# Routing the first part of a mixture-of-experts kernel over six token columns instead of eight

## The chip, the cores and the metric

The kernel runs on one core of one Trainium2 chip. The metric is the device time of one execution in microseconds (us). Three executions of the kernel before took 511.5, 511.85 and 511.92 us; their median is 511.85 us. A profile is a further execution, recorded instruction by instruction; its own time is given beside its span, which runs from the first to the last instruction.

The engines are named as in the profile: PE is the matrix engine (TensorE), with PEld for its weight loads; DVE is VectorE, ACT is ScalarE, POOL is GpSimd, and SP is the engine whose queue issues most transfers.

## The reference

There are 4096 tokens of 256 numbers (64 rows of 64 tokens), eight experts, and two experts chosen for each token. Cut to what matters:

```python
var = jnp.mean(x * x, axis=-1, keepdims=True)
xn = rms_w * (x * jax.lax.rsqrt(var + EPS))
gate = xn @ wg_W + wg_b + (genre_embed @ gg_W + gg_b)
gate_w = jax.nn.softmax(gate, axis=-1)
topk_w, topk_i = jax.lax.top_k(gate_w, TOP_K)          # TOP_K = 2 of E = 8
cw = jnp.sum(jax.nn.one_hot(topk_i, E) * topk_w[..., None], axis=-2)
h1 = jax.nn.relu(jnp.einsum('bsh,ehm->bsem', x, W1) + b1)      # 256 -> 512
h2 = jax.nn.relu(jnp.einsum('bsem,emn->bsen', h1, W2) + b2)    # 512 -> 512
out_e = jnp.einsum('bsen,enh->bseh', h2, W3) + b3              # 512 -> 256
x = x + jnp.einsum('bseh,bse->bsh', out_e, cw)
```

The reference computes all experts for all tokens. Only the two chosen experts of a token have a weight other than zero, so 8192 pairs of token and expert matter.

## The kernel before, in words

**Layout.** Partition p of the 128 holds tokens 32p to 32p+31. Token column i is the i-th token of every partition, that is 128 tokens; there are NI = 32 columns, in groups of TPB = 4, and NG = 8 groups. x is loaded in groups: `load_x(j)` brings group j into `big`. Six groups fit at once; the last two go where groups 0 and 1 were, once these have been used.

**Sorting into tiles.** The pairs are sorted by expert into tiles of BT = 128 pairs, each tile of one expert. A tile is then computed by a gather of its rows of x (an indirect transfer on POOL), three layers on PE with ACT's activations between them, and a scatter that adds the weighted result to the output rows.

**Two parts.** Finding the tiles of all tokens takes long, so the kernel routes the first NA = 8 columns alone first (part A: 1024 tokens, 2048 pairs). From these, each expert gets one first tile of 128 pairs, listed in `idxA`. While PE computes these eight first tiles (`head_step`, one tile each), DVE routes the other NB = 24 columns (part B), and puts what is left of part A and all of part B into the remaining tiles, listed in `idxR`. How many of them are needed depends on the data: 56 to 69, and the last few are behind a switch. A tile in `idxR` is one of a pair of equal expert (two tiles at once, 256 columns on PE) or a single one.

**The front, in the order of the program** (`first_part`). Everything is written in program order under a manual schedule: each engine takes its instructions in the order in which the code names them, and waits are put in from what reads and writes which tile. A PSUM bank (`PB[k]`) counts as one object in this.

1. x groups 0 and 1 are loaded, transposed on PE (`turn`: `turn_pe` writes a bank, `turn_copy` copies it to SBUF on ACT or DVE). `squares(i, eng)` sums the squares of column i into `ss[:, i]`, on ACT (L185) or DVE (L187). Of the eight columns, ACT takes 2, 3, 6, 7 and DVE takes 0, 1, 4, 5. Column 6 stands ahead of the copy of the fourth transposed block on ACT, column 7 behind it.
2. `gates_2` multiplies the transposed columns by the gate weights on PE (L227). ACT copies the result to `gTs` (L448).
3. `pA.norm` makes one over the root mean square from `ss` (L288 to L299, with the square root on ACT, L290).
4. `upright_2` turns the gates so that tokens stand on partitions again, into bank `PB[4]` (L233), four columns to each half. ACT then copies a transposed block (L209), converts half of a table of numbers to float16 (`row_numbers`, L245), and copies three more transposed blocks of the later groups.
5. `pA.choose` is a chain of DVE operations. It reads the bank and multiplies by `rstd` (L308), adds the condition's gates (L315), finds the largest and second largest of each token with a scan (L322), an equality (L331), a difference (L334) and a masking (L337), and counts the pairs along a partition (L342, `incA`). Each works on n·E = 8·8 = 64 elements per partition.
6. `pA.ranks` adds the counts over the partitions on PE (L348, L349), DVE makes each pair's place in its expert's list (L476, L358, L360, `lo16A`).
7. Places are turned to token numbers by one-hot matmuls: 16 columns (2 choices by 8 token columns) in four groups of four, DVE makes each group (L484, `ohA`), PE uses it (L488). DVE makes `idxA` of the result (L492, L493).
8. `gather(0)` on POOL (L712) fetches the first tile's rows; PE transposes them (L767) and starts layer one (L831). On SP, the loads of the weights from the third of expert 0 on wait for this gather (`other_loads`), so that the first tile's rows go first.

**Part B** (`rest`) is a generator. `head_step` takes pieces of it between the steps of the first tiles; its DVE lines are those of part A with n = 24. The two copies of L539 and L544 bring its gates from PSUM into `graw` (32 columns by 8), from which `pB.choose(None)` multiplies.

**Other users of NA.** The sums of squares of the later columns are taken from the list `left`; the weights of the pairs go to `cwdA` (part A; the other columns of it are filled with zeros early, L422) and `cwdR`; and the output is first filled with x: columns 0 to NA-1 in one transfer (L509), the others in four (L929), so that scatters of the first eight tiles may start early.

Of the kernel before, what the change touches and what calls it, by code (L numbers as in the profile page):

```python
# [10 lines left out]
F16 = mybir.dt.float16  # L11
# [10 lines left out]
def kernel(  # L22
# [28 lines left out]
    MC = M // P  # L51
    REP = P // B
    TOPK = 2
    NA = 8
    GA = NA // TPB
    NB = NI - NA
    BT = 128
    SQ = 32
# [22 lines left out]
    def buf(pool, shape, name, dt=F32):  # L81
        return pool.tile(shape, dt, tag=name, name=name)
# [77 lines left out]
    def t2(name, n, dt=F32):  # L160
        return buf(gx, [P, n], name, dt)
# [90 lines left out]
    class Part:  # L252
# [48 lines left out]
        def choose(self, raw):  # L301

            gate, left, rstd = self.gate, self.pr[:, 0], self.t["rstd"]
            if raw is None:
                V.tensor_tensor(gate, graw[:, self.i0 : self.i1, :], self.over_e(rstd), ALU.mult)
            else:
                q = raw.shape[1]
                V.tensor_tensor(  # L308
                    gate.rearrange("p (q k) e -> p q k e", q=q),
                    raw,  # L310
                    self.over_e(rstd).rearrange("p (q k) e -> p q k e", q=q),
                    ALU.mult,
                )
            yield
            V.tensor_tensor(gate, gate, self.over_i(ggate), ALU.add)  # L315
            yield
            gf = gate.rearrange("p i e -> p (i e)")
            tops = (self.pr[:, 1], self.cw8.rearrange("p i e -> p (i e)"))
            ms = []
            for k, (g, top) in enumerate(zip((gf, left), tops)):  # L320

                V.tensor_tensor_scan(  # L322
                    top, fresh[:, 0 : self.n].rearrange("p i e -> p (i e)"), g, 0.0, ALU.add, ALU.max
                )
                top = top.rearrange("p (i e) -> p i e", e=E)
                m = top[:, :, E - 1]
                ms.append(m)
                yield
                if k == 0:
                    nc.gpsimd.tensor_tensor(self.w, gate, self.over_e(m), ALU.subtract)  # L330
                V.tensor_tensor(self.same[:, :, 1:], top, self.over_e(m), ALU.is_equal)  # L331
                yield
                oh = self.ohe[:, k].rearrange("p e i -> p i e")
                V.tensor_tensor(oh, self.same[:, :, 1:], self.same[:, :, 0:E], ALU.subtract)  # L334
                yield
                if k == 0:
                    V.scalar_tensor_tensor(  # L337
                        left.rearrange("p (i e) -> p i e", e=E), oh, -BIG, gate, ALU.mult, ALU.add
                    )
                    yield  # L340

            V.tensor_tensor_scan(self.inc[:, 1:], self.oh[:, 0], self.oh[:, 1], 0.0, ALU.add, ALU.add)  # L342
            V.tensor_tensor(self.t["d2"], ms[1], ms[0], ALU.subtract)
# [34 lines left out]
            nc.gpsimd.dma_start(cwd.rearrange("(p i) e -> p i e", p=P)[:, i0 : i0 + cw8.shape[1], :], cw8)  # L378

    pA, pB = Part("A", 0, NA), Part("B", NA, NI)  # L380
    lo16A = t2("lo16A", GC, F16)
    mvA = buf(gx, [P, GC, E], "mvA", F16)
    totA, totA1 = te("totA"), t2("totA1", E + 1)
    sa, sb = t2("sa", NREST), t2("sb", NREST)

# [9 lines left out]
            loads.append(nc.sync.dma_start(dst, src))  # L395


    left = [NA + i for i in (0, 1, 4, 5, 2, 3, 6, 7)] + list(range(NA + 8, NI))

    def some(n):  # L400
        for _ in range(n):
# [2 lines left out]
    def first_part():  # L404


        rw2 = gTs[0:HC, 0:P]
        load_x(0)
        nc.scalar.dma_start(wg_in, wg_W.rearrange("(c p) e -> p c e", p=P))
        load_x(1)  # L410
        nc.scalar.dma_start(rw2, rms_w.rearrange("(c p) -> c p", c=HC))
        load_x(2, 2)
        nc.scalar.dma_start(gg_sb[0:G, :], gg_W)
        load_x(4, 2)
        nc.scalar.sqrt(warm, ones[:, 0:E])
        V.memset(wg_sb, 0.0)
        V.memset(condT[G : G + 2, :, :], 1.0)
        V.memset(cw8B, 0.0)
        for k in range(3):
            V.memset(ring(run, [P, H], "xg", 3, k), 0.0)  # L420
        V.memset(cgR, 0.0)
        nc.gpsimd.dma_start(cwdA.rearrange("(p i) e -> p i e", p=P)[:, NA:NI, :], cw8B[:, NA:NI, :])  # L422
        busy(7)
        rwp, cps, gps = PB[7][:, P : P + HC], PB[7][0:G, 2 * P : 2 * P + B], PB[7][:, 3 * P : 3 * P + E]
        nc.tensor.transpose(rwp, rw2, ident[:HC, :HC])
        V.tensor_copy(rwT, rwp)
        for c in range(HC):
            V.tensor_scalar(wg_sb[:, c, 0:E], wg_in[:, c, :], rwT[:, c : c + 1], None, ALU.mult)
        for i in (2, 3):
            squares(i, "A")  # L430
        turn(0, 0, 0, "V", 0)
        turn(0, 1, 1, "A", 1)
        squares(0, "V")
        turn(1, 0, 2, "V", 2)
        squares(TPB + 2, "A")
        turn(1, 1, 3, "A", 3)
        squares(TPB + 3, "A")
        nc.tensor.transpose(cps, cond_sb, ident[:B, :B])
        for i in (1, TPB, TPB + 1):
            squares(i, "V")  # L440
        V.tensor_copy(condT[0:G], cps.unsqueeze(2).to_broadcast([G, B, REP]))
        for j in range(NG - GA, NG):
            load_x(j)
        nc.sync.dma_start(vecs[0 : E * MC, :], b1.rearrange("e (c p) -> (e c) p", p=P))
        nc.sync.dma_start(vecs[E * MC : 2 * E * MC, :], b2.rearrange("e (c p) -> (e c) p", p=P))
        load_weights(0, (0, 1))
        gates_2(((0, 1), (2, 3)), PB[3])
        nc.scalar.copy(gTs, PB[3])  # L448
        pA.norm(True)
        turn(GA, 0, 0, "A", 0)  # L450
        nc.tensor.matmul(gps, lhsT=condT.rearrange("g b r -> g (b r)"), rhs=gg_sb, start=True, stop=True)
        V.tensor_copy(ggate, gps)
        row_numbers(0)
        chosen = pA.choose(upright_2(PB[4]))
        for q in (1, 2, 3):
            turn(GA + q, 0, q, "A", q)
        turn_pe(GA, 1, 0)
        next(chosen)
        turn_pe(GA + 1, 1, 4)
        for _ in chosen:  # L460
            pass
        pA.ranks()
        V.tensor_tensor(
            mvA.rearrange("p (k i) e -> p k i e", k=TOPK),
            pA.ohe.rearrange("p k e i -> p k i e"),
            toka.unsqueeze(1).unsqueeze(3).to_broadcast([P, TOPK, NA, E]),
            ALU.mult,
        )
        row_numbers(1)
        pA.exps()  # L470
        gates(0, range(4))
        turn_pe(GA + 2, 1, 1)
        turn_copy(0, "A", 0)
        turn_copy(1, "A", 4)
        turn_copy(2, "A", 1)
        V.scalar_tensor_tensor(  # L476
            pA.slot, pA.inc[:, 1:].rearrange("p (e i) -> p e i", e=E), -1.0, pA.along(pA.adj), ALU.add, ALU.add
        )
        pA.pick(lo16A.rearrange("p (k i) -> p k i", k=TOPK))
        tabA = PB[7][:, 0:E]  # L480
        GH = GC // 4
        for g0 in range(0, GC, GH):
            hs = slice(g0, g0 + GH)
            V.tensor_tensor(  # L484
                ohA[:, :, hs], iotx[:, :, hs], lo16A[:, hs].unsqueeze(1).to_broadcast([P, P, GH]), ALU.is_equal
            )
            for g in range(g0, g0 + GH):
                nc.tensor.matmul(tabA, lhsT=ohA[:, :, g], rhs=mvA[:, g, :], start=(g == 0), stop=(g == GC - 1))  # L488
        pA.totals()
        turn(GA + 3, 1, 3, "A", 2)  # L490

        V.tensor_scalar(sa[:, 0:E], tabA, 0.0, float(NT), ALU.is_equal, ALU.mult)  # L492
        V.scalar_tensor_tensor(idxA, tabA, float(OFFA), sa[:, 0:E], ALU.add, ALU.add)  # L493
        V.tensor_copy(totA1, pA.tot)

    def other_loads():
# [9 lines left out]
        load_weights(1, (0,))  # L506
        nc.sync.dma_start(b3_sb[:, 0:2], b3[0:2].unsqueeze(0).to_broadcast([P, 2, H]))
        load_weights(1, (1, 2))
        fills.append(nc.sync.dma_start(our[:, 0:NA, :], xr[:, 0:NA, :]))  # L509
        load_weights(2)  # L510
        nc.sync.dma_start(b3_sb[:, 2:E], b3[2:E].unsqueeze(0).to_broadcast([P, E - 2, H]))
        for e in range(3, E):
# [21 lines left out]
    def third_part():  # L534

        turn(GA + 5, 1, 7, "V", 3)
        some(len(left))
        raw = upright()
        nc.scalar.copy(graw[:, NA : NA + 4 * TPB, :].rearrange("p (q k) e -> p q k e", q=4), raw)  # L539
        gates_2(((4, 5), (6, 7)), PB[7])  # L540
        nc.scalar.copy(gTs, PB[7])

    def last_upright():
        nc.scalar.copy(  # L544
            graw[:, NA + 4 * TPB : NI, :].rearrange("p (q k) e -> p q k e", q=2), upright_2(PB[6])
        )

    mms = []
# [346 lines left out]
    def head_step(u, more):  # L895
# [29 lines left out]
            give(u - 1)  # L925

        if u >= E - 1 - NF:
            i = NA + (u - (E - 1 - NF)) * (NB // NF)
            fill = nc.sync.dma_start(our[:, i : i + NB // NF, :], xr[:, i : i + NB // NF, :])  # L929
            for a in adds:  # L930
                tc.declare_no_dep(fill.ins, a.ins, reason="the first E tiles hold tokens of the first part alone")
            fills.append(fill)
# [127 lines left out]
```

## Time and profile before

| What | Value |
|---|---|
| runs: lowest, median, highest | 511.5, 511.85, 511.92 us |
| profiled execution: its time, its span | 513.2 us, 511.4 us |
| granted PE clock, mean | 0.995 |
| PE busy, share of the span | 495.6 us, 97% |
| DVE, ACT, POOL busy | 239.2 us (47%), 167.3 us (33%), 288.9 us (56%) |
| gathers of tiles listed in `idxR` (L712) | 59 |
| gathers of tiles listed in `idxA` (L712) | 8 |
| first matmul of layer one (L831) | at 22.97 us |
| last scatter issued (L868) | at 502.02 us |

Rows of the timeline give the start of an instruction, its length, its engine and line, what it writes and reads, and its shape. What stands in brackets at the end is how long the engine was idle before it and what ended the idle time ("<-PE pb L233": a matmul of line 233 that wrote `pb`; "issue": nothing that the profile shows). "x4" behind a row means that four instructions were merged, and the length is then that of all. Rows of a wait list give the waiting engine and line, what it waited for, the total in us, how often, and the longest.

### The profile page before, as it was taken

The numbers are of one execution on the slowest core, as the hardware profiler recorded it, in microseconds if no ns is written. First come the engines' busy times: TensorE is split into PE (matmuls) and PEld (weight loads), VectorE is DVE, ScalarE is ACT, GpSimd is POOL, SyncE is SP. The second block draws the span as 40 slices with busy tenths as digits, with TensorE's granted clock in tenths as the row PEclk, the third lists the DMA queues.
The fourth block names the chain that finished last, engine by engine and source line by source line (L and its number), as shares of the span: only waits on it lengthen the run. The fifth ranks groups of instructions, "written<-read, shape, count | busy, mean of one in ns | idle before, by whom it ended". The sixth has DMA issues, their size and how long they took to land. (4 is left out here: it accounts for less than half of the span.)

```text
span 511.4 us, 8669 instructions
## 1 busy us (share of the span) xinstructions
PE 495.6 (97%) x2840; PEld 445.4 (87%) x2840; DVE 239.2 (47%) x587; ACT 167.3 (33%) x394; POOL 288.9 (56%) x229
## 2 busy tenths in 40 slices
PE   7899999999999999999999999999999999999992
PEld 6679999888888888888888888888888889999991
DVE  5895977244444334334333444443333335655550
ACT  5734444322222222222222222222222222444340
POOL 3455517766666656655556556666565545764621
PEclk9999999999999999999999999999999999999997
DMA  8699996454433343333433344433343333434201
GB/s 326 203 378 393 388 382 204 88 104 80 88 72 79 72 79 77 73 68 75 83 75 76 81 82 84 79 69 80 77 82 64 61 64 53 93 61 77 42 3 23
DMA packets 68257, 59.26 MB, mean 116 GB/s; under 512 B 39615, under 2 KB 59298, under 8 KB 67812
## 3 DMA queue, kind: packets, MB, share of 16 engines
q1 hardware_dynamic: 52608, 41.21, 24.6%
q0 software_dynamic: 15232, 17.34, 21.0%
q8 instruction: 25, 0.41, 0.3%
q14 instruction: 36, 0.29, 0.2%
q10 hardware_dynamic: 356, 0.01, 0.0%
HBM read 42.80 MB, written 20.71 MB: 124 GB/s over the span
## 5 line engine op out<-in xcount | busy, mean ns | idle before, releaser
L842 PE MATMUL pb<-hid,big 128*128 128x256 f32 (+1 forms) x1120 | 210.8, 346 | 0.0
L842 PEld LDWEIGHTS pb<-hid,big 128*128 128x128 f32 x1120 | 187.0, 191 | 20.4
L868 POOL DMA_INDIRECT out_dram<-y,idxR x59 | 97.8, 1658 | 127.9 <-issue 73.1
L845 ACT ACTIVATE hid<-pb,bb 128x256 f32<-128x256 f32 (+1 forms) x140 | 61.5, 440 | 245.7 <-PE pb L842 233.0
L797 DVE COPY big<-w2a 128x2048 f32 x35 | 44.7, 1278 | 160.4 <-PE pb L842 154.9
L831 PE MATMUL pb<-xT,big 128*128 128x256 f32 (+1 forms) x560 | 108.2, 346 | 0.0
L858 PE MATMUL pb<-big,hid 128*128 128x256 f32 x472 | 107.6, 379 | 0.0
L831 PEld LDWEIGHTS pb<-xT,big 128*128 128x128 f32 x560 | 93.5, 191 | 9.9
L858 PEld LDWEIGHTS pb<-big,hid 128*128 128x128 f32 x472 | 88.8, 190 | 11.6
L712 POOL DMA_INDIRECT big<-in_x_dram,idxR x59 | 78.8, 1336 | 20.7 <-issue 17.1
L712 POOL DMA_INDIRECT cg<-cwdR,idxR x59 | 69.0, 1169 | 18.0 <-issue 18.0
L834 ACT ACTIVATE hid<-pb,bb 128x256 f32<-128x256 f32 (+1 forms) x140 | 61.5, 440 | 40.9 <-PE pb L831 26.9
L867 DVE SCALAR_TENSOR_TENSOR y<-pb,cw,bc 128x256 f32<-128x256 f32 x59 | 28.5, 483 | 46.6 <-issue 26.2
L792 DVE COPY big<-w1a 128x1024 f32 x35 | 24.3, 695 | 25.5 <-PE pb L831 22.9
L842 PEld LDWEIGHTS pb<-hid,w2a 128*128 128x128 f32 x256 | 29.9, 192 | 2.3 <-issue 2.0
L842 PE MATMUL pb<-hid,w2a 128*128 128x128 f32 x256 | 30.7, 277 | 0.9 <-issue 0.9
L868 POOL DMA_INDIRECT out_dram<-y,idxA x8 | 15.7, 1963 | 25.1 <-DVE denB L370 7.8
L801 DVE COPY big<-w3a 128x1024 f32 x35 | 25.8, 737 | 2.8 <-issue 2.8
L816 DVE TENSOR_SCALAR bc<-b_sb,cw 128x256 f32 x59 | 22.9, 389 | 2.1
L756 DVE STREAM_TRANSPOSE xT<-gTs 128x256 f32<-128x256 f32 x57 | 22.5, 424 | 0.7 <-DMA gTs<-scr 0.7
L845 ACT ACTIVATE hid<-pb,vT 128x128 f32<-128x128 f32 x32 | 11.4, 367 | 25.3 <-PE pb L842 23.7
L831 PE MATMUL pb<-xT,w1a 128*128 128x128 f32 x128 | 16.0, 278 | 0.0
(224 smaller groups left out, 252.2 us busy)
## 6 DMA issues: line engine op xcount, KB each, us to landing
w2a<-in_L_cond_W_dram SPq DMA_DIRECT2D x8, 1024.0 KB
scr<-big SPq DMA_DIRECT2D x57, 128.0 KB
gTs<-scr SPq DMA_DIRECT2D x228, 32.0 KB
w1a<-in_L_cond_W_dram SPq DMA_DIRECT2D x8, 512.0 KB
w3a<-in_L_cond_W_dram SPq DMA_DIRECT2D x8, 512.0 KB
out_dram<-in_x_dram SPq DMA_DIRECT2D x4, 768.0 KB
big<-in_x_dram SPq DMA_DIRECT2D x4, 512.0 KB
big<-in_x_dram SPq DMA_DIRECT2D x2, 1024.0 KB
```

Source lines behind the costliest of these rows:

```text
L712: return nc.gpsimd.indirect_dma_start(out=dst, out_offset=None, in_=src, in_offset=bass.IndirectOffsetOnAxis(ap=index(b), axis=0), bounds_ ...
L792: V.tensor_copy(st1, w1a[:, e].rearrange("p e c m -> p (e c) m"))
L797: V.tensor_copy(st2, w2a[:, ex[u]].rearrange("p e c m -> p (e c) m"))
L801: V.tensor_copy(st3, w3a[:, ex[u]].rearrange("p e c m -> p (e c) m"))
L816: V.tensor_scalar(bc, b3e, cw, None, ALU.mult)
L831: nc.tensor.matmul(ph, lhsT=w1[:, c, ts(m, P)], rhs=cols[:, c, :], start=(c == 0), stop=(c == HC - 1))
L834: nc.scalar.activation(hids[:, 0, m, 0 : w * BT], ph, AF.Relu, bias=bb[:, 0, m : m + 1])
L842: nc.tensor.matmul(ph, lhsT=w2[:, m, ts(n, P)], rhs=hids[:, 0, m, 0 : w * BT], start=(m == 0), stop=(m == MC - 1))
L845: nc.scalar.activation(hids[:, 1, n, 0 : w * BT], ph, AF.Relu, bias=bb[:, 1, n : n + 1])
L858: nc.tensor.matmul(po, lhsT=hids[:, 1, n, ts(k, BT)], rhs=w3[:, n, :], start=(n == 0), stop=(n == MC - 1))
L867: V.scalar_tensor_tensor(y, sums(b), cw, bc, ALU.mult, ALU.add)
L868: add = nc.gpsimd.indirect_dma_start(out=orows, out_offset=bass.IndirectOffsetOnAxis(ap=index(b), axis=0), in_=y, in_offset=None, bounds_c ...
```

## The change

The first part routes NA = 6 columns. Its groups are still GA = 2, and NX = GA·TPB = 8 is the number of columns that the first two groups hold. Columns 6 and 7 are loaded, transposed and multiplied by the gate weights with the first six, as before, but they belong to part B, which has NB = 26 columns.

- The squares of columns 6 and 7 stay on ACT, and both stand behind the copy of the fourth transposed block.
- The gates of columns 6 and 7 lie in the same bank as those of the first six. A new ACT copy brings them (16 elements per partition) into `graw`. In the code it stands ahead of the first operation of `pA.choose`, because that is a generator, whose first piece runs at `next(chosen)`; on ACT it stands behind `row_numbers(0)`.
- The first multiplication of `choose` reads six columns, which are not a multiple of four, and is made in two pieces, of four columns and of two.
- The one-hot columns are GCA = 12 instead of 16, in three groups of four.
- What is about loaded groups and not about routing (the list `left`, the later copies to `graw`, the fills of the output) uses NX, and so stays as it was.

```diff
-    NA = 8
-    GA = NA // TPB
+    NA = 6
+    GA = -(-NA // TPB)
+    NX = GA * TPB
+    GCA = TOPK * NA
...
-                q = raw.shape[1]
-                V.tensor_tensor(
-                    gate.rearrange("p (q k) e -> p q k e", q=q),
-                    raw,
-                    self.over_e(rstd).rearrange("p (q k) e -> p q k e", q=q),
-                    ALU.mult,
-                )
+                for i in range(0, self.n, TPB):
+                    k = min(TPB, self.n - i)
+                    V.tensor_tensor(
+                        gate[:, i : i + k],
+                        raw[:, i // TPB, 0:k],
+                        rstd[:, i : i + k].unsqueeze(2).to_broadcast([P, k, E]),
+                        ALU.mult,
+                    )
...
-    lo16A = t2("lo16A", GC, F16)
-    mvA = buf(gx, [P, GC, E], "mvA", F16)
+    lo16A = t2("lo16A", GCA, F16)
+    mvA = buf(gx, [P, GCA, E], "mvA", F16)
...
-    left = [NA + i for i in (0, 1, 4, 5, 2, 3, 6, 7)] + list(range(NA + 8, NI))
+    left = [NX + i for i in (0, 1, 4, 5, 2, 3, 6, 7)] + list(range(NX + 8, NI))
...
-        squares(TPB + 2, "A")
         turn(1, 1, 3, "A", 3)
-        squares(TPB + 3, "A")
+        for i in range(NA, NX):
+            squares(i, "A")
         nc.tensor.transpose(cps, cond_sb, ident[:B, :B])
-        for i in (1, TPB, TPB + 1):
+        for i in [1] + list(range(TPB, NA)):
             squares(i, "V")
...
-        chosen = pA.choose(upright_2(PB[4]))
+        raw = upright_2(PB[4])
+        chosen = pA.choose(raw)
+        nc.scalar.copy(graw[:, NA:NX], raw[:, GA - 1, NA % TPB :])
...
-        for g0 in range(0, GC, GH):
+        for g0 in range(0, GCA, GH):
...
-                nc.tensor.matmul(tabA, lhsT=ohA[:, :, g], rhs=mvA[:, g, :], start=(g == 0), stop=(g == GC - 1))
+                nc.tensor.matmul(tabA, lhsT=ohA[:, :, g], rhs=mvA[:, g, :], start=(g == 0), stop=(g == GCA - 1))
...
-        fills.append(nc.sync.dma_start(our[:, 0:NA, :], xr[:, 0:NA, :]))
+        fills.append(nc.sync.dma_start(our[:, 0:NX, :], xr[:, 0:NX, :]))
...
-        nc.scalar.copy(graw[:, NA : NA + 4 * TPB, :].rearrange("p (q k) e -> p q k e", q=4), raw)
+        nc.scalar.copy(graw[:, NX : NX + 4 * TPB, :].rearrange("p (q k) e -> p q k e", q=4), raw)
...
-            graw[:, NA + 4 * TPB : NI, :].rearrange("p (q k) e -> p q k e", q=2), upright_2(PB[6])
+            graw[:, NX + 4 * TPB : NI, :].rearrange("p (q k) e -> p q k e", q=2), upright_2(PB[6])
...
-            i = NA + (u - (E - 1 - NF)) * (NB // NF)
-            fill = nc.sync.dma_start(our[:, i : i + NB // NF, :], xr[:, i : i + NB // NF, :])
+            i = NX + (u - (E - 1 - NF)) * ((NI - NX) // NF)
+            fill = nc.sync.dma_start(our[:, i : i + (NI - NX) // NF, :], xr[:, i : i + (NI - NX) // NF, :])
```

The number of tiles behind the first eight is the sum over the experts of (pairs of the expert, less those in its first tile) over 128, rounded up. It stays the same as long as no expert has too few pairs in the first part to fill its first tile.

## The prediction

> **What bounds the kernel now.** I read the busy time by stage first: where TensorE is full, only its own work counts.
>
> ```profile
> 0.00:23.00 23.00, 18.34 (x129) 13.63 (x129) 15.49 (x72) 14.53 (x31) 8.18 (x23) 1.00 0.73 270
> 23.00:100.00 77.00, 76.05 (x599) 71.80 (x600) 55.54 (x149) 32.70 (x90) 41.36 (x37) 1.00 0.89 307
> ...
> 400.00:495.00 95.00, 95.00 (x681) 90.26 (x680) 47.85 (x98) 36.20 (x96) 51.62 (x35) 1.00 0.32 60
> ```
>
> Columns: stage, length, busy us of PE, PE loads, DVE, ACT, POOL, then granted clock, DMA share, GB/s. From 100 us on PE is busy 100%; between 23 and 100 us it misses 0.95 us; the last 10 us are the last tile's scatter. So the time is: start of the first expert matmul (22.97 us), plus PE work fixed by the number of tiles, plus 0.95 us, plus a fixed end. The change edits the front. The waits of PE, second view, name who holds it there.
>
> ```profile
> PE pb L842 <- issue: 0.9, 1, 0.9
> PE pb L348 <- DVE d2A L343: 0.8, 1, 0.8
> PE pb L767 <- DMA xg<-in_x_dram,idxA: 0.7, 1, 0.7
> ```
>
> PE waits for DVE's choice (L348) and for the gather of the first tile (L767), which needs `idxA`. Third view, the timeline: start, length, engine, line.
>
> ```profile
> 10.91 1.05 ACT L245 CAST iotx<-hotA 128x1024 f16<-128x1024 f32 x1
> ...
> 11.69 0.23 DVE L308 TENSOR_TENSOR gateA<-pb,rstdA 128x64 f32<-128x64 f32 x1 [0.23 <-PE pb L233]
> 11.95 0.23 DVE L315 TENSOR_TENSOR gateA<-gateA,ggate 128x64 f32<-128x64 f32 x1
> ...
> 14.30 0.29 DVE L342 TENSOR_TENSOR_SCAN incA<-ohA 128x64 f32<-128x64 f32 x1
> ...
> 14.65 0.39 PE L348 MATMUL pb<-incA,tri 128*128 128x8 f32 x2 [0.81 <-DVE d2A L343]
> ...
> 16.44 1.44 DVE L484 TENSOR_TENSOR hotA<-iotx,lo16A 128x512 f16<-128x512 f16 x4
> ...
> 17.01 1.34 PE L488 MATMUL pb<-mvA,hotA 128*128 128x8 f16 x16 [0.16 <-DVE hotA L484]
> ...
> 18.59 0.17 DVE L493 SCALAR_TENSOR_TENSOR idxA<-pb,sa 128x8 int32<-128x8 f32 x1
> ...
> 19.04 1.12 POOL L712 DMA_INDIRECT xg<-in_x_dram,idxA  x1 [6.12 <-DVE denA L369]
> ...
> 22.00 0.50 PE L767 MATMUL pb<-ident,xg 128*128 128x128 f32 x2 [0.72 <-DMA xg<-in_x_dram,idxA]
> ...
> 22.97 2.05 PE L831 MATMUL pb<-xT,w1a 128*128 128x128 f32 x16
> ```
>
> This is one chain without slack: uprights on PE (end 11.66) → DVE's gate multiply → choice → ranks → one-hots → `idxA` → gather, 2.96 us in flight → first layer. What shortens or delays it moves everything behind, since the weight loads on SP from 21.98 on wait for this same gather.
>
> **The two squares on ACT: nothing.** In the old order the square of column 6 runs at 7.31 and the copy of the fourth transposed block starts at 8.12 after 0.30 us of waiting for PE; the square did not delay it. Both squares now follow the copy. A square's pitch is 0.54 us (4.63 to 5.17), so they run from 8.61 to about 9.66; the gate copy L448 cannot start before 9.85, when PE's gates are done. That wait (0.73 us before) hides them; without it each would cost 0.54. The column-7 square also releases the seventh x load on SP: 9.66 instead of 9.11, but that load already waits for DVE's square ending at 9.65, and its data are used at 19.20.
>
> **The new copy `graw` and the wait it makes: +0.40 us.** The copy reads the bank that DVE's gate multiply reads (PB[4]). In the built program the multiply waits no longer for PE but for this ACT copy, and the copy stands in ACT's queue behind the 1.05 us cast at 10.91. The old row speaks for a start at 11.69, right behind PE.[...] ACT rows overlap by about 0.1 (L209 at 10.44 for 0.58, cast at 10.91), so the copy starts about 11.86. Its length is 0.17 to 0.21: 0.27 for 128 elements (L539), 0.21 for 64 (L544) and for 8 (L415). It ends at about 12.05; from ACT to DVE took 0.03 at L290 to L291; start 12.09: **+0.40**, bounds +0.33 to +0.5. Behind the copy on ACT stand three block copies, held until 12.13 by PE anyway, hence at most 0.05 late, and not used by PE before 15.19. PE's fifth block of transposes also waits for this bank: free about 12.4, PE gets there near 13.4.
>
> **The multiply in two pieces: +0.04.** Two unlinked short DVE operations start 0.06 to 0.1 apart (14.51 to 14.57; 18.59 to 18.67). First piece 0.10, second 0.17 long, 0.03 to its reader: 0.30 against 0.26 (11.69 to 11.95).
>
> **Six columns instead of eight: -0.72.** 64 elements become 48. Slopes come from the same lines in part B (192 elements) and from 8-element rows (0.15 to 0.16 long). L315: 0.23 to 0.36, 1.0 to 1.3 ns an element, 16 to 21 ns saved. Scans (0.29 to 0.56): 34 ns, three. L331 (0.22 to 0.36): 18 ns, two. L334 (0.28 to 0.63) 35 to 44 ns, two. L337 (0.27 to 0.61) 33 to 42 ns. Sum to `incA`: about 0.28. Behind the ranks: L476 17 ns, L358 34 ns, L360 58 to 87 ns (0.39 for 128, 1.09 for 384): 0.12. `mvA` saves 0.03 beside PE's ranks, worth nothing. Of four one-hot groups (1.44, so 0.36 each) one goes: 0.36; PE's groups of four (1.34 by 4: 0.34) follow at DVE's pace. PE is not in the way: its transposes at 16.19 shift with the ranks by +0.40+0.04-0.28 = +0.16 to 17.01, the first group is ready at 17.05. Together -0.76, of which I keep -0.72, as PE is within 0.04 of being last there.
>
> **Sum: +0.40 + 0.04 - 0.72 = -0.28 us.** `idxA`, gather 0, first expert matmul: 22.97 to about 22.7.
>
> **Part B grows by two columns: nothing.** Its DVE lines get 16 elements each, about 0.28 in the choice and 0.2 in slots; part A's second placing gives 0.2 back. Cover: DVE idles 4.89 us at L578 (47.12) for PE, and the first table one-hots end near 61.0 while PE uses them at 63.45. Tile 0's result (41.47) stands behind the choice and is late by 0.28; behind it POOL's scatter and the gather of tile 5 (44.17), used by PE at 57.91. Without that cover each 0.1 is 0.1.
>
> **DMAs and queues: nothing.** SP issues the same loads in the same order and sizes. The weight table writes 48 columns instead of 64, its zero fill 208 instead of 192; POOL's three products for it are shorter by a few tens of ns. DMA share is 0.00 to 0.18 between 19 and 21 us, so an earlier gather meets no traffic.
>
> **Tiles: unchanged.** Counting the reference's choices on its inputs, each expert finds at least 128 tokens in six columns (172 243 166 221 203 172 129 230), so every first tile stays full and 59 tiles remain behind, as the page shows (x59).
>
> **The time.** The profiled execution took 513.2: span 511.4 and 1.8 around it. It becomes 511.1 and 512.9. The runs' median, 511.85, lies 1.35 below that execution; the same step gives **511.55**. From no change a measurement here tells about 0.2%, 1.02 us, so the forecast is "no difference".
>
> **Rivals.**
>
> ```profile
> 37.30 0.37 ACT L834 ACTIVATE hid<-pb,vT 128x128 f32<-128x128 f32 x1 [1.07 <-PE pb L842]
> ...
> 37.72 3.17 PE L842 MATMUL pb<-hid,w2a 128*128 128x128 f32 x26 [0.95 <-issue]
> ```
>
> 1. **The 0.95 us stall goes.** In the second tile ACT's four activations run at 33.69, 35.13, 35.87 and 37.30 though PE had finished by 34; PE then waits for the fourth. DMA share is about 1 there. If an ACT program shifted by one instruction and loads 0.3 earlier avoid it: -0.28-0.95, 510.6. For: PE's work leaves no reason for it. Against: the loads keep their order, and the three runs agree within 0.42 us.
> 2. **The wait eats more than the columns give.** If the copy runs behind the block copies' wait (start 12.13) and takes 0.27, and PE's transposes hold the one-hots: +0.55, +0.04, -0.4: 512.05. If the stall of rival 1 also doubles, 513.0. Against: the copy's turn and its PE count are ahead of those block copies.
> 3. **A first tile is not full.** Then 60 tiles instead of 59, at the end's single-tile pitch of 7.08 us (layer one at 485.16 and 492.24): 518.6. It decides when expert 6 has 126 or fewer in six columns; 767 choices in all less 126 need six tiles instead of five. By the count it has 129; the average is 192 (1536 choices by 8). Near, but counted.
> 4. **The columns save, and the wait is hidden**: -0.68, 511.17. Against: DVE waited only for PE before and has no other work ahead of the multiply.
>
> **How the numbers follow.** Forecast 0.70; rival 1 0.11; rival 2 0.10; rival 3 0.03; rival 4 0.06. The forecast's own bounds (wait 0.33 to 0.5, columns 0.6 to 0.8) give 511.35 to 511.85 with 0.2 of spread of a median. The range 510.6 to 512.3 takes in rivals 1, 2 and 4, and leaves out rival 3 and a doubled stall. Faster by over 0.2% is nearly all of rival 1: 0.10. Slower by over 0.2% is rival 3 and the far end of rival 2: 0.08. Within: 0.82.
>
> **What would show it.** In the profile after: the gate multiply starting near 12.1 with an ACT releaser; `incA` about 0.16 later than 14.30; three one-hot groups of 0.36; `idxA` near 18.3; first expert matmul near 22.7; the gate copy of ACT still at 9.85; x59 gathers; PE busy 100% beyond 100 us. A multiply at 11.7, squares that push the gate copy, a first matmul at 23 or later, or another idle time of PE between 23 and 100 us would make the prediction wrong.

## The result, and the profile after

| | Median | Lowest to highest | Runs |
|---|---|---|---|
| before | 511.84 us | 511.05 to 512.94 | 10 |
| after | 513.58 us | 512.77 to 513.9 | 10 |

The ratio is 1.0029, 95% interval 1.0021 to 1.0038: the kernel became 1.7 us slower, where no difference was forecast. The profiled execution after took 513.9 us with a span of 512.2.

The stages of the kernel after, in the columns used before (busy us of PE, PE loads, DVE, ACT, POOL, then granted clock, DMA share, GB/s):

```profile
0.00:23.00 23.00, 18.08 (x124) 13.42 (x124) 14.69 (x72) 14.42 (x31) 8.05 (x23) 1.00 0.74 269
23.00:100.00 77.00, 75.34 (x599) 70.85 (x597) 56.47 (x149) 33.21 (x91) 41.83 (x36) 1.00 0.92 307
...
400.00:495.00 95.00, 95.00 (x681) 90.28 (x680) 48.55 (x99) 35.88 (x95) 53.13 (x36) 1.00 0.33 60
```

PE now misses 1.66 us between 23 and 100 us. Behind that nothing changed. The waits of PE after say who holds it:

```profile
PE pb L772 <- DMA big<-in_x_dram,idxR: 1.6, 1, 1.6
PE pb L351 <- DVE d2A L346: 1.0, 1, 1.0
PE pb L772 <- DMA xg<-in_x_dram,idxA: 0.7, 1, 0.7
```

The first row is new: PE waits for the gathers of tiles 8 and 9, the first pair listed in `idxR`. The row of 0.9 us for "issue" (L842 before) is gone. The timeline of the front after:

```profile
10.36 0.59 ACT L451 COPY gTs<-pb 128x512 f32<-128x512 f32 x1 [0.19 <-PE pb L229]
...
11.43 1.05 ACT L247 CAST iotx<-hotA 128x1024 f16<-128x1024 f32 x1
...
12.38 0.18 ACT L459 COPY graw<-pb 128x16 f32<-128x16 f32 x1
12.59 0.27 DVE L311 TENSOR_TENSOR gateA<-pb,rstdA 128x32 f32<-128x32 f32 x2 [0.63 <-ACT graw L459]
...
17.03 1.10 DVE L489 TENSOR_TENSOR hotA<-iotx,lo16A 128x512 f16<-128x512 f16 x3
...
18.84 0.17 DVE L498 SCALAR_TENSOR_TENSOR idxA<-pb,sa 128x8 int32<-128x8 f32 x1
```

These are the forecast's steps: the multiply waits for ACT's copy, the copy runs behind the cast, three one-hot groups instead of four, and the gate copy L451 still waits for PE, so the two squares ahead of it cost nothing. The whole front of this execution stands some 0.5 us later than in the profiled execution before. This is not of the change: PE starts the first transposes 0.19 us later (5.02 against 4.83), and does them at a pitch of 0.21 us, before it goes over to 0.11, for longer (until 8.3 us instead of 7.4); `b_again` lies between the two. To take that out, the times are read from the end of the uprights on PE (L233 before, L235 after), over all traces of this study:

| From the end of the uprights, us | Eight columns (9 traces) | Six columns (7) | Six columns, multiply ahead of the copy (4) |
|---|---|---|---|
| gate multiply starts | 0.04 | 0.41 to 0.42 | 0.04 |
| `idxA` starts | 6.92 to 6.94 | 6.66 to 6.67 | 6.28 to 6.29 |
| first expert matmul starts | 11.28 to 11.41 | 11.01 to 11.09 | 10.68 to 10.77 |

So the front became some 0.26 us shorter (medians 11.30 and 11.04), as forecast. The loss is elsewhere. PE of the kernel after, around the new wait:

```profile
82.89 1.89 PE L863 MATMUL pb<-w3a,hid 128*128 128x256 f32 x8
86.42 0.86 PE L772 MATMUL pb<-ident,big 128*128 128x128 f32 x4 [1.63 <-DMA big<-in_x_dram,idxR]
```

And the same place in another profiled execution of the kernel before (`b_again`, span 510.3):

```profile
82.89 1.89 PE L858 MATMUL pb<-w3a,hid 128*128 128x256 f32 x8
84.62 0.73 PE L767 MATMUL pb<-ident,big 128*128 128x128 f32 x4
```

PE comes to this place at the same time in both, and goes on 1.80 us later in the kernel after. The span is 1.9 us longer. The wait is the loss.

### The profile page after: what moved, and what is told of

It reads as the page before. It is cut to its first block, busy times and chain, and to the rows that moved or that the text cites. A ratio compares the mean times of both kernels' runs of the same rounds, so it can differ in the third digit from the quotient of the medians.

```text
span 512.2 us, 8662 instructions
## 1 busy us (share of the span) xinstructions
PE 495.5 (97%) x2836; PEld 444.9 (87%) x2836; DVE 238.9 (47%) x587; ACT 168.0 (33%) x395; POOL 290.8 (57%) x229
## 5 line engine op out<-in xcount | busy, mean ns | idle before, releaser
L847 PE MATMUL pb<-hid,big 128*128 128x256 f32 (+1 forms) x1120 | 210.8, 346 | 0.0
L847 PEld LDWEIGHTS pb<-hid,big 128*128 128x128 f32 x1120 | 187.0, 191 | 20.4
L847 PEld LDWEIGHTS pb<-hid,w2a 128*128 128x128 f32 x256 | 29.7, 192 | 1.1 <-issue 0.8
L847 PE MATMUL pb<-hid,w2a 128*128 128x128 f32 x256 | 30.3, 276 | 0.0
```

What stands on the lines that cost most here:

```text
L847: nc.tensor.matmul(ph, lhsT=w2[:, m, ts(n, P)], rhs=hids[:, 0, m, 0 : w * BT], start=(m == 0), stop=(m == MC - 1))
```

## The experiments

### What holds the gathers: the first theory

The first theory was a chain. The result of tile 0 (`give(0)`) is 0.7 us later than in the profiled execution before, POOL's scatters follow one another, and the gathers of tiles 8 and 9 stand behind them. The rival was the transfers: the gathers land when SP's stream of weights and output fills has run dry. Four kernels tell them apart: the kernel before again (`b_again`); six columns with the gate multiply ahead of the copy (`a_mulfirst`); and six and eight columns with `give(0)` and `give(1)` right behind `layer3` (`a_early`, `b_early`).

```diff
 # a_mulfirst
         chosen = pA.choose(raw)
+        next(chosen)
         nc.scalar.copy(graw[:, NA:NX], raw[:, GA - 1, NA % TPB :])
...
-        next(chosen)
 # a_early and b_early
             layer3(u - 1)
+            if u <= 2:
+                give(u - 1)
...
-        if u >= 1:
+        if u >= 3:
             give(u - 1)
```

> The kernel before, profiled once more. Chain theory (the gather of the first tile behind the eight first tiles, issued on POOL behind five scatters that wait for each other, sets the time): the 0.95 us that PE waited near 37 us in the first profile is an accident that the chain hides in part, so without it PE waits for that gather (L767 with a DMA releaser, 0.3 to 1 us) and the execution is 0.5 to 1.4 us below 513.2. Rival (PE's stream alone sets the time): no wait of PE behind 38 us, and the time falls by the stall that is missing and no more.

> The six-column kernel with DVE's gate multiply ahead of ACT's graw copy: the multiply waits for PE again, ACT's copy for DVE. Both theories expect idxA 0.35 to 0.45 us earlier. Chain theory: DVE is busy without a pause from idxA to the first tile's result, so the first scatter and the end come 0.4 earlier: 513.2. Rival (the scatters land at times that the weight traffic sets, whatever their start): less than 0.2.

> The six-column kernel with the results of tiles 0 and 1 written directly behind their third layer, the first of them ahead of the rest of part B's choice on DVE. Chain theory: the first scatter starts near 39 instead of 42.9, the chain of scatters and with it the gather behind them come at least 1.6 us earlier, PE's wait of 1.63 us at the first paired tile goes, time -1.3 to -1.7: about 512. Rival (the first matmul's start decides): no change, 513.5.

> The same reordering in the kernel before. Chain theory: whatever PE waits at the first paired tile goes, -0.2 to -1.0, and the two kernels with this order differ only by their fronts, within 0.3 us. Rival (PE's stream alone sets the time): 0.

| | Median, us | Ratio to before (512.12), 95% | PE at the pair's rows | Its wait |
|---|---|---|---|---|
| b_again | 511.99 (one) | | 84.62 | none |
| b_early | 512.10 | 0.9995, 0.9982 to 1.0008 | 84.82 | none |
| a_mulfirst | 512.84 | 1.0012, 1.0002 to 1.0022 | 85.45 | 1.35 |
| a_early | 513.14 | 1.0019, 1.0010 to 1.0029 | 84.74 | 0.70 |

The chain theory fails. It has one thing for it: the first gather of the pair is issued at 81.46 in the kernel after and at 79.11 in `b_again`. But tile 0's result came at 41.42 us in `a_early`, against 42.16 after, the eight-column kernel gained nothing, and both six-column kernels wait although their gathers are issued earlier still: the first at 76.68 in `a_early` and 78.47 in `a_mulfirst`. `a_mulfirst` stands 0.7 above before where the kernel after stands 1.7 above it; neither theory expected a gain of that size. The scatter ahead of these gathers, issued between 74.8 and 79.4 us, landed between 84.1 and 86.1 in all of them, within 1 us behind the last packet of the stream (`a_early`, where it landed 1.7 us ahead of it, is the exception). The transfers of the kernel after, by stage (last columns: DMA share, GB/s):

```profile
25.00:75.00 50.00, 50.00 (x428) 47.65 (x428) 42.47 (x117) 22.75 (x64) 23.53 (x19) 1.00 1.06 373
...
80.00:84.00 4.00, 4.00 (x34) 3.87 (x33) 2.83 (x8) 2.21 (x6) 3.39 (x3) 1.00 1.01 337
```

And of `b_again`:

```profile
25.00:75.00 50.00, 50.00 (x428) 47.64 (x428) 42.05 (x117) 22.76 (x64) 22.35 (x19) 1.00 1.06 381
...
80.00:84.00 4.00, 4.00 (x34) 3.87 (x33) 2.78 (x8) 2.21 (x6) 3.08 (x4) 1.00 0.90 281
```

The engines of the core do the same work, the DMA engines are full in both (share 1.06 between 25 and 75 us), but they move 2% less in the kernel after (373 GB/s against 381), and they are still full at 80 to 84 us (1.01) where the kernel before begins to run dry (0.90). Call "the stream" what SP moves from its first waiting load (`w3a` of expert 0) to the last packet of the fills. It lasts 60.66 and 60.93 us before and in `b_again`, and 62.84 after; the executions before and after have the same number of packets and bytes.

### Why the same transfers take longer: the addresses

What differs is where they are written. The constant tile `fresh` has NB columns, so it grew from 24 x 8 to 26 x 8 floats, by 64 bytes for each partition (`toka` shrank from 32 to 24 bytes; the five tiles below moved by 64 in all). Everything allocated behind it in SBUF moved. The start addresses of the five large tiles that take loads and gathers, in bytes within a partition:

```
        w1a     w2a     w3a     big     hid
before  34304   67072   132608  165376  189952   (all multiples of 512)
after   34368   67136   132672  165440  190016   (64 past a multiple of 512)
```

Four kernels tell the shift from the six columns: the six-column kernel with one 64-byte tile put elsewhere, so that the five tiles are where they were; the eight-column kernel with a gap of 64 bytes, and of 256; and the first with the multiply ahead as well. The gap brings one short memset at the start with it. In `a_align` all engines run the same instructions in the same order as in the kernel after.

```diff
 # a_align (and a_mul_align)
-    tok16 = const.tile([P, NI], F16, name="tok16")
...
+    tok16 = buf(gx, [P, NI], "tok16", F16)
 # b_pad64; 64 instead of 16 in b_pad256
     iot = const.tile([P, NREST], F32, name="iot")
+    gap = const.tile([P, 16], F32, name="gap")
+    V.memset(gap, 0.0)
```

> The six-column kernel, with the same instructions in the same order; only the 64-byte tile tok16 lies elsewhere, so that w1a, w2a, w3a, big and hid start at multiples of 512 bytes in SBUF again, as before the change (behind it they start 64 bytes later). Address theory: the stretch from SP's first w3a load to the last fill packet goes from 62.8 us back to 60.7-61.2 (some 366 GB/s), the waits of PE for the gathers of the first paired tiles go from 1.6 us to below 0.3, and the time is 511.7-512.3, that is 1.3 to 1.8 below the changed kernel. Rival (the six columns' own work or transfers slow the stage): stretch 62.5 or more, PE wait 1 us or more, 513.2-513.9.

> The eight-column kernel of before with a gap of 64 bytes in SBUF ahead of the weights, so that w1a, w2a, w3a, big and hid start 64 bytes past a multiple of 512; nothing of the routing is changed. Address theory: stretch of the loads and fills 62.5-63.2 us instead of 60.7-61.0, PE waits 0.8-1.8 us at the gathers of the first paired tiles, time 1.0 to 1.8 us above before (512.9-513.6). Rival (the six columns themselves): within 0.3 of before.

> The eight-column kernel of before with a gap of 256 bytes, so that the same tiles start 256 bytes past a multiple of 512. Address theory with a boundary of 256 bytes or less[...]: as before, stretch 60.7-61.2, within 0.3 of before. Address theory with a boundary of 512 bytes: as with the gap of 64. Rival (any move of the tiles costs, or none does): the same as the gap of 64 bytes, whichever that gives.

> The six-column kernel with the gate multiply ahead of the graw copy, and with the tiles at multiples of 512 bytes again. If address and the order of the copy are the two terms that decide: first expert matmul 0.4-0.7 earlier than before's, no PE wait over 0.3 at the first paired tiles, 511.2-511.7, that is 0.2 to 0.7 below before. Rival (the stage is bound by its transfers whatever the front does, so an earlier front is given back): the same as before within 0.2, with a wait of PE of the size that the front gained.

The stream answered at once; the times did not. In three later sessions, on three chips, all kernels, that of before too, ran near 518 us, and the comparisons of the medians say nothing:

| | Stream, us | Median | before | Ratio, 95% |
|---|---|---|---|---|
| a_align | 60.05 | 518.20 | 518.04 | 0.9999, 0.9975 to 1.0022 |
| b_pad64 | 62.82 | 517.16 | 518.04 | 0.9986, 0.9960 to 1.0012 |
| b_pad256 | 61.25 | 518.84 | 518.04 | 1.0018, 0.9997 to 1.0039 |
| a_mul_align | 60.45 | 517.95 | 518.04 | 1.0001, 0.9979 to 1.0024 |
| a_again | 62.08 | 518.69 | 517.93 | 1.0019, 1.0000 to 1.0038 |
| a_align2 | 60.42 | 518.17 | 517.93 | 1.0015, 0.9995 to 1.0036 |
| b_pad64_2 | 62.44 | 518.48 | 517.93 | 1.0004, 0.9982 to 1.0025 |
| a_mul_align2 | 60.32 | 517.90 | 517.93 | 1.0008, 0.9987 to 1.0029 |
| a_align3 | 61.19 | 518.05 | 517.68 | 1.0013, 0.9989 to 1.0037 |
| b_pad64_3 | 62.39 | 518.36 | 517.68 | 1.0014, 0.9980 to 1.0047 |
| a_mul_align3 | 59.94 | 516.64 | 517.68 | 0.9966, 0.9935 to 0.9998 |

The stream separates without exception: 59.94 to 61.25 us in the kernels without the shift of 64 bytes, 62.08 to 62.82 in those with it, whether they have six columns or eight. The expected times did not come. The few low executions don't show them either: in the third session the lowest were 512.48 before, 512.39 in `b_pad64_3` with the shift and 513.65 in `a_align3` without it.

> The changed kernel once more, on the same chip as the three beside it. In the run before this one, ACT's activations of the second tile came up to 5 us late and TensorE's clock then fell to 0.5 for some 4 us, in all kernels alike, so that PE came too late to wait for transfers; the times tell nothing where that happens. Where it does not: stretch from the first w3a load to the last fill 62.5-63.1 us, PE waits 1-1.7 us at the first paired tiles, 1.2-2.0 us above before.

> The six-column kernel with the tiles at multiples of 512 bytes again. Address theory: stretch 60.0-61.2, no PE wait above 0.3 at the first paired tiles, within 0.4 of before and 1.0-1.8 below the changed kernel. Rival (the six columns themselves): the same time as the changed kernel within 0.4.

> The eight-column kernel with the tiles 64 bytes past a multiple of 512. Address theory: stretch 62.5-63.1 (it was 62.82 in the run before this one), PE waits 0.8-1.8 at the first paired tiles, 0.9-1.8 above before. Rival: within 0.3 of before.

> Six columns, gate multiply ahead of the graw copy, tiles at multiples of 512 bytes. If the stretch of loads is short enough, PE's work sets the time: first expert matmul 0.6-1.0 earlier than in before, time 0.3-1.0 below before and below a_align2. Rival (the transfers bound the stage): within 0.2 of before, with a PE wait of 0.4 or more at the first paired tiles.

> The six-column kernel with the tiles at multiples of 512 bytes again, once more, in the hope of executions in which ACT's second tile is not held up. There the address theory has it within 0.4 of before, with no PE wait above 0.3 at the first paired tiles and a stretch of 60.0-61.2; the rival (the six columns themselves) has it 1.2-1.8 above before. Where ACT is held up by 3 us or more, PE comes after the transfers anyhow and both theories give the time of before within the scatter.

> The eight-column kernel with the tiles 64 bytes past a multiple of 512. Where ACT is not held up: address theory 0.9-1.8 above before, stretch 62.4-63.1, PE waits 0.8-1.8 at the first paired tiles; rival within 0.3 of before. Where ACT is held up by 3 us or more: the same as before by both.

> Six columns, gate multiply ahead of the graw copy, tiles at multiples of 512 bytes. Where ACT is not held up: if PE's work sets the time, 0.4-1.0 below before; if the transfers bound the stage again, within 0.2 of before with a PE wait of 0.4 or more at the first paired tiles.

The reason shows in the traces. PE and ACT of `a_align` in the second tile:

```profile
34.72 0.37 ACT L839 ACTIVATE hid<-pb,vT 128x128 f32<-128x128 f32 x1 [1.33 <-PE pb L772]
...
37.60 0.37 ACT L839 ACTIVATE hid<-pb,vT 128x128 f32<-128x128 f32 x1 [2.51 <-PE pb L847]
...
38.02 0.49 PE L847 MATMUL pb<-hid,w2a 128*128 128x128 f32 x2 [1.67 <-issue]
...
40.51 0.62 ACT L839 ACTIVATE hid<-pb,vT 128x128 f32<-128x128 f32 x2 [2.55 <-remote]
...
40.93 1.43 PE L847 MATMUL pb<-hid,w2a 128*128 128x128 f32 x5 [2.42 <-ACT hid L839]
```

And its stages there (third column from the end: granted clock):

```profile
38.00:40.00 2.00, 0.49 (x2) 0.30 (x2) 1.93 (x3) 0.00 (x0) 1.67 (x2) 0.98 1.04 398
40.00:42.00 2.00, 1.07 (x5) 1.07 (x6) 1.90 (x5) 1.29 (x4) 0.00 (x0) 0.50 1.13 423
42.00:44.00 2.00, 2.00 (x11) 2.00 (x11) 0.76 (x5) 0.41 (x2) 1.20 (x1) 0.50 0.99 401
44.00:46.00 2.00, 2.00 (x12) 2.00 (x10) 0.00 (x0) 0.66 (x2) 1.49 (x2) 0.50 1.03 407
```

ACT's activations of the second tile come 2.9 us apart, though the matmuls that they need had ended at 34.2. PE idles 4.1 us (1.67 and 2.42), and its granted clock is then 0.50 for 6.8 us (3.4 us in two of the other traces). In all but one of the profiles of these sessions PE comes to the first pair at 88.6 to 91.9 us instead of 84.6 and waits for no gather, so the stream's length cannot show in the time. This hold-up of ACT has the form of the 0.95 us stall in the profiled execution before, grown; `b_again` and the kernel after don't have it.

The exception is `b_pad64`, eight columns with the shift, which the expectation of `a_again` overlooks. There the stall took 1.6 us, the granted clock stayed at 1.00 (36 to 48 us), and PE came to the pair at 86.69 and did not wait. But its transfers are as late as those of the kernel after: the stream ends at 85.03 us (85.10 after, 82.63 and 83.19 before and in `b_again`), and the last 1 KB packet of the scatter that stands ahead of the gathers ends at 85.54 (85.70 after, 83.31 and 83.79 before and in `b_again`). So the shift alone makes these transfers late, without the six columns. An unstalled PE would have come at 85.1 (an estimate: 86.69 less 1.6), ahead of that packet; that the wait then follows is not seen here.

### Making the stream end last

The last three kernels were meant to make the stream the last to end in every execution: six more copies of 0.75 MB behind SP's last fill, from x to rows in HBM that nobody reads.

```diff
 # b_more; the same on b_pad64 (b_more_pad64) and on the kernel after (a_more)
             fills.append(fill)
+            if u == E - 2:
+                for s in spare:
+                    nc.sync.dma_start(s[:, :, :], xr[:, i : i + 6, :])
```

> The eight-column kernel of before with six more copies of 0.75 MB (x into spare rows in HBM, results not used) behind SP's last fill, 4.5 MB or some 12 us of transfers. The gathers of the first paired tiles then land near 97 us, later than PE comes even where ACT's second tile is held up, so that the length of the stream sets the time in every execution. Both theories: 5 to 12 us above an undisturbed before, with PE waits of 4 us or more at the first paired tiles and a scatter of the times of under 1 us.

> The same with the 64-byte gap, so that w1a, w2a, w3a, big and hid start 64 bytes past a multiple of 512. Address theory: 1.4 to 2.6 us above b_more, the 2 us by which the stream of weights is longer. Rival (the shift costs nothing by itself, the six columns do): within 0.4 of b_more.

> The changed six-column kernel, which has the shift, with the same 4.5 MB. Address theory: as b_more_pad64 within 0.6 us (the front differs by some tenths), so 1.2 to 2.6 above b_more. Rival (the six columns cost by themselves, through their rows or part B): above b_more_pad64 by 1 us or more.

| | Median (6 runs) | Lowest to highest | Last fill or copy ends |
|---|---|---|---|
| b_more | 518.83 us | 518.13 to 520.56 | 101.0 us |
| b_more_pad64 | 521.65 us | 520.18 to 522.95 | 102.8 us |
| a_more | 521.87 us | 519.89 to 524.05 | 102.9 us |

Beside them before ran at 511.89. With these copies the shift alone costs 2.8 us, a little more than the 1.4 to 2.6 expected; the six columns on top of it 0.2. With six runs each and this scatter, the 1 us that the rival gave to the columns is not excluded here. The rows of PE in `b_more`, at the first pair and at the second:

```profile
88.63 0.70 PE L768 MATMUL pb<-ident,big 128*128 128x128 f32 x2 [3.27 <-DMA big<-in_x_dram,idxR]
89.87 0.71 PE L768 MATMUL pb<-ident,big 128*128 128x128 f32 x2 [0.53 <-DMA big<-in_x_dram,idxR]
...
108.00 3.62 PE L832 MATMUL pb<-xT,big 128*128 128x256 f32 x16
```

In `b_more_pad64`:

```profile
86.59 0.50 PE L770 MATMUL pb<-ident,big 128*128 128x128 f32 x2 [1.35 <-DMA big<-in_x_dram,idxR]
87.33 0.51 PE L770 MATMUL pb<-ident,big 128*128 128x128 f32 x2 [0.24 <-DMA big<-in_x_dram,idxR]
109.28 5.09 PE L834 MATMUL pb<-xT,big 128*128 128x256 f32 x16 [4.15 <-DVE xT L759]
```

And in `a_more`:

```profile
87.28 0.51 PE L773 MATMUL pb<-ident,big 128*128 128x128 f32 x2 [2.46 <-DMA big<-in_x_dram,idxR]
88.33 0.70 PE L773 MATMUL pb<-ident,big 128*128 128x128 f32 x2 [0.54 <-DMA big<-in_x_dram,idxR]
110.01 6.26 PE L837 MATMUL pb<-xT,big 128*128 128x256 f32 x16 [4.17 <-DVE xT L762]
```

The 2.8 us do not arise at the first pair: there both kernels with the shift went on earlier than `b_more`. They arise at the second pair, whose rows reach PE over SP's queue, behind the copies (`xT` from `stow` and `shuffle`). DVE has these rows ready at 107.59 us in `b_more` and at 109.14 in `b_more_pad64`, 1.55 later, about the 1.8 us by which the stream ends later. So the second pair starts 1.3 us later (109.28 against 108.00); the wait reads 4.15 because PE had come there sooner. Behind the wait the granted clock is 0.50 for 3.4 us, and the third pair starts 2.75 later (124.57 against 121.82). So in these runs the longer stream cost time where PE waited for what stood behind it, but at another wait than that of the kernel after.

The 12 us for the copies were an estimate: 4.7 MB at the 381 GB/s of `b_again` take 12.4. The last copy of `b_more` ended at 101.0 us, 17.8 behind the end of the stream in `b_again` (83.19). The landing near 97 us, the waits of 4 us at the first pair and the scatter below 1 us did not come: the first pair was let go at 87 to 89 after waits of 1.6 to 3.8 us in all, and the runs scatter by 2.4 to 4.2 us. The scatter ahead of the gathers landed 9.5 to 10.8 us behind its issue, while the stream went on for another 13 to 17 us. So here it did not wait for the end of the stream, but took some 10 us beside a full one (DMA share 0.99 to 1.03 between 80 and 100 us). In `b_again` and in the kernel after it took 6.9 and 6.6, and there the stream ended meanwhile (83.19 and 85.10). That fits a landing set by the end of the stream there and not here; it was not tried apart.

## Why the prediction was wrong

**The failed step is "DMAs and queues: nothing".** It checked that SP issues the same loads in the same order and sizes, and never where they are written. Shown: the shift of 64 bytes makes the stream longer with eight columns too, undoing it makes the six-column stream as short as before (60.05 to 61.19 us instead of 62.84), and with eight columns and the shift the scatter ahead of the gathers is as late as after. The term put at nothing cost a wait of 1.63 us at the first pair, which is as large as the loss and larger than the 0.26 us gained in the front.

**The reading that hid it: "where TensorE is full, only its own work counts".** The first view gave 0.89 as DMA share between 23 and 100 us, and in `b_again` the first gather of the pair landed at 84.47, 1.3 us behind the end of the stream. PE took its rows at 84.62: there was 0.15 us to spare. In the profiled execution before, its stall brought PE there only at 85.82 and so hid how close this was. The stage had two bounds nearly level, and the sum counted one. The listed signs held this one: another idle time of PE between 23 and 100 us.

**The wait of the multiply: right.** +0.40 forecast, +0.37 to +0.38 measured (0.04 to 0.41 or 0.42), and the copy 0.17 to 0.18 long, inside 0.17 to 0.21. `a_mulfirst` confirms that it is the order that costs it: with the multiply ahead, `idxA` comes another 0.38 earlier. After the change the multiply starts 0.03 us behind the copy's end (12.59, 12.56). Whether the two could read the bank at once, no run here tried.

**The columns: right.** The first expert matmul moved by -0.26 against -0.28.

**The squares, part B, the tiles: right.** L451 still waits 0.19 for PE. No wait of PE in part B is new. The remaining gathers are again x59.

**The 0.95 us stall of rival 1** belongs to the execution and not to the kernel: `b_again` doesn't have it. It is the greater part of the 1.36 us by which that execution lay above the others' median. The forecast carried this distance over as a constant and so came out at the right level.

**What stays open.** No execution of `a_align` without ACT's hold-up was profiled, so that its return to the time of before is inferred from its stream and from the late transfers of `b_pad64`, not seen in its time. `a_mul_align` has the front 0.6 us shorter and no shift; in the three sessions it stood at 1.0001, 1.0008 and 0.9966 to before, and only the last interval (0.9935 to 0.9998) leaves out 1, which is too little to call it faster. What holds up ACT was not found. In `a_early` the stream was 64.40 us long and the wait only 0.70; the scatter ahead of its gathers was issued early enough (74.81) to land at 84.21, ahead of the stream's end. That execution took 512.48, 0.4 above that of `b_early`; why the median stands 1.0 above before is not explained.

## What to carry to other kernels

A change of a shape can move the tiles that are allocated behind it, here by 64 bytes; where the DMA engines are full (share 1.06 here), compare the tiles' addresses before and after. In the three later sessions the stream took 59.94 to 61.25 us with the targets of the large transfers at multiples of 512 bytes or 256 past one, and 62.08 to 62.82 with them 64 past one; placing one small tile elsewhere was enough to undo the shift. When one engine is busy all through a stage, still ask what the DMA share is and how long ahead of its use the last transfer lands: here a second bound 0.15 us behind the first was enough to lose a gain of 0.26. And profile the kernel before twice: the second trace shows whether a stall belongs to the kernel or to one execution.

## What the runs showed of the hardware

**With the large SBUF tiles 64 bytes past a multiple of 512, the loads were slower, in part of their packets.** Times of SP's packets between 23 and 80 us, over 11 traces without and 9 with the shift:

| Packet | Median, both | 90th percentile without | with the shift |
|---|---|---|---|
| 1 KB | 46 ns | 46 | 58 |
| 2 KB | 84 to 86 ns | 84 | 95 to 98 |
| 4 KB | 159 to 161 ns | 159 | 173 to 182 |

Without the shift 91 to 98% of the packets take the usual 46, 84 or 159 ns, or 1 ns more. With it only 61 to 66% of the 1 KB ones do, and 47 to 56% of the others; the rest spread over longer times. The 6 KB packets of the fills, which go from HBM to HBM and were not moved, have a median of 234 ns without the shift and 234 to 239 with it (kernels without the added copies); over all 640 of them in one execution the 90th percentile is 264 ns before and 276 after. With the gap of 256 bytes the stream took 61.25 us and moved 390 GB/s between 25 and 75 us; with the gap of 64 it took 62.82 and moved 373. So the short stream did not need multiples of 512 here; a gap of 128 was not tried.

The 90th percentiles with the shift are 58/46 = 1.26, 95/84 = 1.13 and 173/159 = 1.09 times those without, and up to 98/84 = 1.17 and 182/159 = 1.14. But the packets spread between the usual time and that one, and the stream took some 3% longer (62.84 us against 60.66 and 60.93). By what mechanism the address that is written makes a packet slower was not shown.

**After 4.1 us of PE's idle time in `a_align` its granted clock was 0.50; after waits of some 1.6 us in other runs it was 1.00 or 0.56.** In `a_align`, after 1.67 and 2.42 us without work, the granted clock was 0.50 for 6.8 us, which costs some 3.4 us of PE's work (an estimate: half of 6.8); 28 matmuls of L847 took 6.15 us there, and 32 took 3.73 at 65.99 us. After the single wait of 1.63 us in the kernel after, after 1.35 us in `a_mulfirst`, and after 1.32 and 0.28 us in `b_pad64`, it stayed at 1.00. But after 1.35 and 0.24 us in `b_more_pad64` it fell to 0.56 and 0.59:

```profile
88.00:90.00 2.00, 2.00 (x13) 2.00 (x12) 0.00 (x0) 0.89 (x2) 1.62 (x1) 0.56 1.01 316
90.00:92.00 2.00, 2.00 (x13) 2.00 (x13) 0.00 (x0) 0.37 (x1) 0.00 (x0) 0.59 0.99 399
```

So in these runs the length of one wait alone (1.35 us in `a_mulfirst` and in `b_more_pad64`) does not tell what clock was granted behind it.
